# Two attention layers in one kernel: where the projection's results are made and stored, and when the second layer's weights are mixed

## The chip, the cores and the metric

The kernel runs on one core of a Trainium2 chip. The metric is the device time of one execution in microseconds (us). The kernel before the change took 3325.8 us, the median of three runs (3324.72, 3326.9 and 3325.8). The profiled execution spans 3324.6 us. All times below are from that profile, and L12 is line 12 of the kernel's source. The engines are named PE (matrix multiplications; PEld is its loading of weights), DVE (vector engine), ACT (activations), POOL (GpSimd) and SP (which issues all DMAs here).

## What is computed

Two layers of the same form, on x of shape 8 x 512 x 32 x 32 (8 images, 512 channels, 1024 positions), all in float32. For each layer and each image:

```python
xn   = groupnorm(x) * gamma + beta                    # 8 groups in layer 0, 32 in layer 1
q, k, v = split(qkv_w @ xn + qkv_b)                   # 1536 x 512 weights, 8 heads of 64
attn = softmax(q.T @ k / sqrt(64))                    # 1024 x 1024 per head
out  = attn @ v
x    = proj_w @ out + proj_b + x                      # the residual
```

The images are independent of one another, and the second layer reads what the first one wrote.

## The kernel before, in words

A unit is one layer of one image. There are 16: units 0 to 7 are layer 0, units 8 to 15 layer 1. The outer loop (L856) goes over the units and interleaves neighbours: it emits the projections of unit u to q, k and v (`projections`, L451), then the output projection of unit u-1 (`project`, L524), then the attention of unit u (`attention`, L610). The stages of one unit are therefore: q, k, v; the output projection of the unit before it; attention, during which the next unit's group norm is worked out piece by piece.

The order of the instructions on each engine is that in which the code emits them; nothing reorders them afterwards. An engine takes its queue in order and stops at an instruction that waits. Waits come from data dependencies and from tile pools: a pool with n buffers makes the writer of a new tile wait until whoever used that buffer last is done with it.

**The projections.** The multiplications by a weight matrix use Strassen's scheme (Winograd's form) with seven products of half-sized blocks in place of eight; `blocks` (L353) is this for q, k, v and o (the output projection). It needs sums of weight blocks, made once per layer by `mix_weights` (L139, four additions or subtractions for each matrix), and sums of the data, made by `mix_right`. In most units three of the seven products (`INNER`) are themselves done by the scheme, with inner left factors made of the weights by `mix_inner_left` (L216), stored in DRAM and loaded at the end of an attention (`load_inner_left`, L237). Units 0 and 8 multiply the output's matrix without this inner scheme; so do q and k of unit 0, and v in every unit.

In `blocks`, intermediate sums live in three tiles of 128 x 2 x 512: p1 (pool `accpool`, tag "acc"), u2 (pool `trpool`, tag "tr") and u3 (for the output projection: pool `rbpool`, tag "rb"). The callbacks finish the four quarters of the result:

- `c11` (L555) makes the first quarter from PSUM and the residual;
- `others` (L562) adds a sum tile to the PSUM bank for each of the other three quarters (on DVE, L565);
- with the inner scheme, `add_rest` (L408) and `rests` (L571) add what the inner products left over, on POOL (L411, L412, L575), after ACT has copied pieces out of PSUM (L396 to L405);
- `done` (L536) adds bias and residual to u2, u3 and p1 (L532).

The residual w.res is four tiles of 128 x 1024 with tag "p" in `ppool`, which has 4 buffers. The same four buffers hold the exponentials of the attention that follows. Results are stored by `store` (L552) in half rows of 256 KB, eight for each unit, from w.res.

**Attention.** 64 steps in 8 chunks of 8 (`c, t = divmod(s, NT)`, L771). Each step has a pair of score products on PE (L643), one exponential on ACT (L651, into a tile "p"), the product of the previous step's exponential with v (L671), and an addition of the exponential to a running sum on DVE (L688 for the first two of a chunk, L690 for the others). A p tile is free again when PE's product and DVE's addition have read it. At the start of a chunk DVE also evacuates and transposes for the one before (L697, L703), a little later it reduces (L713); in chunks 3, 5 and 7 it works out reciprocals (seven small instructions, L730 to L739, at t = 0) and divides (L753, at t = 6). The running sums take tiles of tag "acc" (2 buffers), the transposes tiles of tag "tr" (2 buffers).

**What is hung into the attention.** `at_step` (L910) is called after each step and emits work for the next unit: mean and variance in chunk 1 (with a power on POOL, L298, at t = 5), seven small scale operations on DVE in chunk 2 at t = 0 (L304 to L316), the normalization on ACT in chunks 2 to 5, and sums for the next unit in chunk 6. In unit 0 all of this comes a chunk later (`late`, L908). It also emits the parts of `mix_inner_left`: one part for each of chunks 3, 4 and 5, at t = 0:

```python
            if t == 0 and 3 <= c < 3 + len(left_parts):
                left_parts[c - 3]()
```

The parts exist in units 0 and 7 (q and k of each layer: 24 POOL operations of 128 x 128 and six stores) and 1 and 9 (the output's matrix: half as many).

**The second layer's weights.** In unit 7 (`u == B - 1`, L883) the kernel loads the three matrices of layer 1 (3 MB) as soon as unit 7's q, k and v no longer need those of layer 0, and emits all twelve mixing operations on POOL at once (L885, L886), ahead of the output projection of unit 6 and of attention 7.

## Time and profile before

| engine | busy us | share of the span | instructions |
|---|---|---|---|
| PE | 3273.6 | 98% | 21776 |
| PEld | 1847.7 | 56% | 21776 |
| DVE | 2446.7 | 74% | 2977 |
| ACT | 1583.0 | 48% | 2065 |
| POOL | 903.5 | 27% | 956 |

| group of instructions | count | mean ns |
|---|---|---|
| L643 PE, scores, 64 x 512 | 7808 | 590 |
| L671 PE, products with v, 64 x 512 | 8192 | 590 |
| L651 ACT, exponential, 128 x 1024 | 976 | 1023 |
| L690 DVE, addition of exponentials, 128 x 1024 | 768 | 1240 |
| L688 DVE, the first addition of a chunk | 128 | 1259 |
| L575 POOL, left-over sums, 128 x 512 | 78 | 1270 (median) |
| L886 POOL, mixing of layer 1's weights, 128 x 512 | 12 | 1257 to 1721 |
| L565 DVE, finishing a quarter of the result, 128 x 512 | 90 | 680 |

DMA is light: a mean of 54 GB/s over the span. A store of a half row takes 2.0 us from issue to landing in the median.

How to read such a profile. The page gives the busy time of each engine, the span in 40 slices (each digit a tenth of the slice; PEclk is the clock that PE was granted), and the chain of work that ended last. A matmul's end is modelled from its start, so PE's busy share is not the share of its peak, and a short wait can be hidden under the end of the matmul before it. The view of waits says which engine waited for which instruction, with the sum, the count and the longest. The timeline lists instructions by time: start, duration, engine, line, what is written and read, and in brackets how long the engine had been idle and what released it.

### The profile page before, as it was taken

Reading aid. Unit: us, or ns where it says so; the run is one execution under the profiler, and the core shown is the slowest. Engines: PE = TensorE matmul, PEld = TensorE weight load, DVE = VectorE, ACT = ScalarE, POOL = GpSimd, SP = SyncE. Lnnn points to the kernel's source line nnn. Section 1 sums busy time; section 2 is a strip of 40 time slices with the busy share of each in tenths; the row PEclk is TensorE's granted clock in tenths of the full one; section 3 lists DMA queues with packets and bytes.
Section 4 is the critical chain, followed back from the end, with each engine's and each line's share of the span. In section 5 each row is a group of like instructions: output and inputs, shape, how many; then the busy total and the mean of one; then the engine's idle time right before and its main releaser. Section 6 shows DMA issues by size and latency. Waiting matters only on the chain.

```text
span 3324.6 us, 54851 instructions
## 1 busy us (share of the span) xinstructions
PE 3273.6 (98%) x21776; PEld 1847.7 (56%) x21776; DVE 2446.7 (74%) x2977; ACT 1583.0 (48%) x2065; POOL 903.5 (27%) x956
## 2 busy tenths in 40 slices
PE   8999999999999999997999999999999999999999
PEld 4445465555646556564465554646556565565643
DVE  4876958769586795965958779586795967859577
ACT  1552726436274462733726436274462734537254
POOL 0231051421504214045251411504214042240510
PEclk9999999999999999998999999999999999999999
DMA  2111110121201212013111111201212012120121
GB/s 78 43 46 70 42 72 28 41 78 36 80 24 35 78 35 90 15 35 115 50 71 42 52 58 43 81 24 35 78 36 90 15 34 84 39 80 15 49 83 47
DMA packets 77525, 178.44 MB, mean 54 GB/s; under 512 B 21968, under 2 KB 26192, under 8 KB 77264
## 3 DMA queue, kind: packets, MB, share of 16 engines
q1 hardware_dynamic: 77264, 174.86, 15.6%
q8 instruction: 177, 2.90, 0.4%
q14 instruction: 84, 0.69, 0.1%
HBM read 135.62 MB, written 37.62 MB: 52 GB/s over the span
## 4 chain that ended last, share of the span: by engine, by line
PE 93%; POOL 3%; DVE 1%; DMA 1%; issue 1%; ACT 1%; SPq 0%; ACTq 0%; POOLq 0%; DVEq 0%
PE a L671 25%; PE s L643 24%; PE a L373 17%; PE s L373 15%; PE a L391 5%; PE s L391 5%; POOL x L575 1%; PE a L643 1%; DMA mid<-x 1%; ACT p L651 0%; DVE acc L690 0%; PE s L591 0%; PE a L591 0%; POOL m_o L411 0%; POOL m_o L412 0%
## 5 line engine op out<-in xcount | busy, mean ns | idle before, releaser
L651 ACT ACTIVATE p<-s 128x1024 f32<-128x1024 f32 x976 | 996.8, 1023 | 561.6 <-PE s L643 502.9
L671 PE MATMUL a<-p,v 64*64 64x512 f32 x8192 | 1120.5, 590 | 9.6 <-ACT p L651 8.5
L643 PE MATMUL s<-q,k 64*64 64x512 f32 x7808 | 1077.3, 590 | 1.4 <-DVE v L517 1.4
L690 DVE TENSOR_TENSOR acc<-acc,p 128x1024 f32<-128x1024 f32 x768 | 952.4, 1240 | 88.6 <-ACT p L651 36.2
L671 PEld LDWEIGHTS a<-p,v 64*64 64x64 f32 x8192 | 403.4, 132 | 492.6 <-ACT p L651 362.4
L643 PEld LDWEIGHTS s<-q,k 64*64 64x64 f32 x7808 | 421.6, 133 | 396.5 <-issue 387.9
L866 POOL TENSOR_TENSOR r<-xn 128x256 f32<-128x256 f32 x60 | 75.0, 1250 | 1154.3 <-DVE acc L690 887.7
L688 DVE TENSOR_TENSOR acc<-p,p 128x1024 f32<-128x1024 f32 x128 | 161.2, 1259 | 29.7 <-ACT p L651 29.7
L298 POOL TENSOR_TENSOR y<-var,half 128x4 f32<-128x4 f32 x16 | 32.2, 2014 | 532.6 <-DVE var L296 532.6
L703 DVE STREAM_TRANSPOSE tr<-acc 128x1024 f32<-128x1024 f32 x128 | 157.9, 1234 | 0.0
L713 DVE TENSOR_REDUCE red<-tr 128x32 f32<-128x1024 f32 x128 | 153.8, 1202 | 0.5
L697 DVE TENSOR_TENSOR ao<-a,tmp 128x512 f32<-128x512 f32 x128 | 87.9, 687 | 63.0 <-ACT tmp L696 62.9
L421 ACT COPY p_o<-a 128x1024 f32<-128x1024 f32 x15 | 15.2, 1012 | 244.2 <-PE a L373 244.2
L373 PE MATMUL a<-xn,w 128*128 128x512 f32 x272 | 125.5, 605 | 4.0 <-DVE xn L326 4.0
L373 PE MATMUL s<-xn,w 128*128 128x512 f32 x256 | 115.4, 594 | 1.7 <-DVE xn L170 1.6
L373 PE MATMUL a<-w,xn 128*128 128x256 f32 x512 | 115.7, 379 | 0.0
L373 PE MATMUL a<-x_t,s1w 128*128 128x512 f32 x256 | 115.1, 592 | 0.0
L373 PE MATMUL s<-x_t,s2w 128*128 128x512 f32 x256 | 115.1, 592 | 0.0
L492 POOL TENSOR_TENSOR k<-k,m_k 128x512 f32<-128x512 f32 x90 | 112.3, 1270 | 0.0
L492 POOL TENSOR_TENSOR q<-q,m_q 128x512 f32<-128x512 f32 x90 | 112.0, 1266 | 0.0
L373 PEld LDWEIGHTS a<-w,xn 128*128 128x128 f32 x512 | 97.4, 190 | 13.5 <-issue 0.5
L320 ACT ACTIVATE xn<-xn,shift,scale 128x512 f32<-128x512 f32 x124 | 99.3, 803 | 6.6 <-DVE shift L316 6.6
(241 smaller groups left out, 4236.0 us busy)
## 6 DMA issues: line engine op xcount, KB each, us to landing
rb<-drec SPq DMA_DIRECT2D x128, 256.0 KB, 3.9
xn<-mid SPq DMA_DIRECT2D x36, 512.0 KB, 7.7
il<-il SPq DMA_DIRECT2D x30, 576.0 KB, 4.4
xn<-x_dram SPq DMA_DIRECT2D x32, 512.0 KB, 7.0
x<-x_dram SPq DMA_DIRECT2D x32, 512.0 KB, 4.8
mid<-x SPq DMA_DIRECT2D x64, 256.0 KB, 2.0
x<-mid SPq DMA_DIRECT2D x28, 512.0 KB, 5.0
out_dram<-x SPq DMA_DIRECT2D x56, 256.0 KB, 2.0
```

Source lines behind the costliest of these rows:

```text
L320: nc.scalar.activation(cols, cols, AF.Identity, bias=st["shift"][:, c : c + 1], scale=st["scale"][:, c : c + 1],)
L373: nc.tensor.matmul(dst, at[:, c, ts(i, P)], moving[:, c, :], start=start and c == 0 and not (tokens and i % 2), stop=stop and c == 1, skip ...
L391: nc.tensor.matmul(dst, left[j], right[j], start=start, stop=stop, skip_group_check=True)
L492: w.last[sel].append(nc.gpsimd.tensor_add(cols, cols, rest[:, i, :]))
L643: nc.tensor.matmul(bank[e * H : (e + 1) * H, j, :], w.k[pr][j * H : (j + 1) * H, t * P + e * H : t * P + (e + 1) * H], w.q[pr][j * H : (j ...
L651: exp = nc.scalar.activation(p, bank, AF.Exp, scale=SCALE)
L671: nc.tensor.matmul(banks[r][j * H : (j + 1) * H, :], w.v[rows, t, lo : lo + D], p[rows, j, :], start=(t == 0), stop=(t == NT - 1),)
L688: nc.vector.tensor_add(acc, state["first"], p)
L690: nc.vector.tensor_add(acc, acc, p)
L697: i1 = nc.vector.tensor_add(w.ao[pr // 2][:, pr % 2, ts(qh, FD)], banks[1], tmp)
L703: nc.vector.transpose(tr, state["acc"].pop(c))
L713: nc.vector.tensor_reduce(red[:, :, qh, :], state["tr"].rearrange("p j (f i) -> p j f i", i=BL), AX.X, ALU.add)
```

## The change

It has three parts.

1. `others` writes the finished quarter into the tile that holds the sum (p1, u2 or u3) instead of the residual tile, `rests` adds to it there, and `store` stores from there. The first quarter stays in the residual tiles. The aim is that the residual tiles, whose buffers the attention's exponentials need, don't have to wait for the stores.
2. The twelve mixing operations of layer 1's weights are not emitted at once in unit 7 but put ahead of the inner left factors' parts, to be emitted one at a time from attention 7's steps. The aim is that they do not stand in front of the output projection's work on POOL.
3. The parts are emitted at every second step (t = 0, 2, 4, 6) from chunk 3 on, and from chunk 4 on in unit 0.

```diff
+        results = {}
+
         def store(o, h):
-            nc.sync.dma_start(dst[o * P : (o + 1) * P, ts(h, FD)], w.res[o][:, ts(h, FD)])
+            nc.sync.dma_start(dst[o * P : (o + 1) * P, ts(h, FD)], results[o, h])
 
         def c11(bank):
             for i in range(2):
-                cols = w.res[i][:, :FD]
+                cols = results[i, 0] = w.res[i][:, :FD]
                 plus(cols, i, bank[:, i, :], cols)
...
         def others(r, h, bank, more):
             for i in range(2):
                 o = 2 * r + i
-                w.evac[h] = nc.vector.tensor_add(
-                    w.res[o][:, ts(h, FD)], bank[:, i, :], more[:, i, :]
-                )
+                results[o, h] = more[:, i, :]
+                w.evac[h] = nc.vector.tensor_add(more[:, i, :], bank[:, i, :], more[:, i, :])
...
         def rests(r, h, rest):
             for i in range(2):
                 o = 2 * r + i
-                cols = w.res[o][:, ts(h, FD)]
+                cols = results[o, h]
                 nc.gpsimd.tensor_add(cols, cols, rest[:, i, :])
                 store(o, h)
...
         if u == B - 1:
             lefts, mixing_w = mix_weights(1, load_weights(1), nc.gpsimd)
-            for part in mixing_w:
-                part()
-        left_parts = ()
+        left_parts = []
         if u in (0, B - 1):
             left_parts = mix_inner_left(units[u + 1][0], lefts[:2], inner_left)
+            if u > 0:
+                left_parts = mixing_w + left_parts
         elif u in (1, B + 1):
...
             c, t = divmod(s, NT)
-            if t == 0 and 3 <= c < 3 + len(left_parts):
-                left_parts[c - 3]()
+
+            if left_parts and t % 2 == 0 and c >= 3 + late:
+                left_parts.pop(0)()
```

## The prediction

> **What bounds the kernel now.** The page first. PE is busy for almost the whole span, and the chain that ended last runs over PE, so a gain can only be PE idle time or throttled clock.

> ```profile
> PE 3273.6 (98%) x21776; PEld 1847.7 (56%) x21776; DVE 2446.7 (74%) x2977; ACT 1583.0 (48%) x2065; POOL 903.5 (27%) x956
> PEclk9999999999999999998999999999999999999999
> PE 93%; POOL 3%; DVE 1%; DMA 1%; issue 1%; ACT 1%; SPq 0%; ACTq 0%; POOLq 0%; DVEq 0%
> ```

> POOL's 3% of the chain is odd, and the clock drops in one slice. The waits of PE, longest first, begin with one of 16.3 us, and a small class of 18 waits for exponentials:

> ```profile
> PE a L391 <- ACT m_o L396: 16.3, 1, 16.3
> PE a L671 <- ACT p L651: 8.5, 18, 2.3
> ```

> The timeline around 1530 us (unit 7, when the projection of unit 6 is due) shows the big one. Columns: start, duration, engine, line, tiles, [idle before <- releaser].

> ```profile
> 1516.98 1.27 POOL L886 TENSOR_TENSOR s1w<-w 128x512 f32<-128x512 f32 x1 [12.92 <-DMA w<-qkv_wT_dram]
> 1518.38 3.44 DVE L532 SCALAR_TENSOR_TENSOR u_o<-x,vec,u_o 128x512 f32<-128x512 f32 x2
> ...
> 1535.16 2.48 POOL L575 TENSOR_TENSOR x<-x,m_o 128x512 f32<-128x512 f32 x2
> 1537.67 0.37 ACT L396 COPY m_o<-a 128x256 f32<-128x256 f32 x1 [23.61 <-POOL x L575]
> 1538.09 1.22 PE L391 MATMUL a<-ro,lo 128*128 128x256 f32 x2 [16.28 <-ACT m_o L396]
> ```

> POOL takes its queue in order: the twelve mixing operations of L886 (waiting for weights until 1516.98, ending at 1533.7) stand ahead of the projection's sums (L411, L412, L575), ACT waits for the tile these free, PE for ACT.

> The 18 small waits lie at the starts of attentions. Unit 6:

> ```profile
> 1322.38 1.95 PE L643 MATMUL s<-q,k 64*64 64x512 f32 x16
> 1324.13 2.17 ACT L651 ACTIVATE p<-s 128x1024 f32<-128x1024 f32 x2 [1.28 <-DMA mid<-x]
> 1324.61 2.51 POOL L575 TENSOR_TENSOR x<-x,m_o 128x512 f32<-128x512 f32 x2
> 1328.08 1.02 ACT L651 ACTIVATE p<-a 128x1024 f32<-128x1024 f32 x1 [1.77 <-DMA mid<-x]
> 1329.25 1.09 PE L671 MATMUL a<-p,v 64*64 64x512 f32 x8 [0.28 <-ACT p L651]
> ```

> The first four p tiles are the residual tiles x; each exponential waits for their stores to land. PE's recorded wait is less than its real loss, as busy time is modelled. I therefore took, from the trace, the time from an attention's first score matmul to its 65th L671 matmul (first product of step 8). Units 0, 1 and 9, whose projection has no POOL part or which have none, take 15.47, 15.50, 15.50 us. Units 2 to 8: 16.33, 16.81, 17.15, 17.03, 16.33, 16.93, 17.08; units 10 to 15: 16.30, 16.35, 16.28, 16.34, 16.29, 16.40. Over 15.50 that is 9.2 + 5.0 = 14.1 us.

> [...] in the DVE and POOL timelines at 222 us:

> ```profile
> 222.19 2.48 POOL L492 TENSOR_TENSOR q<-q,m_q 128x512 f32<-128x512 f32 x2
> 222.33 1.19 DVE L734 TENSOR_TENSOR tot<-one,two 32x64 f32<-32x64 f32 x1
> 223.56 0.23 DVE L735 STREAM_TRANSPOSE rows<-tot 32x64 f32<-32x64 f32 x1
> ```

> L734's median is 0.214 us; beside a 128x512 POOL sum it took 1.19, until that ended; the one-input L735 kept its 0.23. [...] Here the clock was 0.63 in 1520 to 1540 us and 0.95 in the next 20 us, and stayed 1.00 around the 2.3 us wait near 144 us.

> **Part 1, weights mixed during attention 7: the removal.** From the projection's first matmul to the first score, unit 6 takes 1299.48 to 1322.38 = 22.90 us, unit 7 1503.60 to 1544.99 = 41.39. With nothing ahead of its POOL sums unit 7 should match unit 6: -18.5 us, 16.3 of it the wait and 2.2 the slow clock. The weights' DMA stays where it is and still lands near 1517.

> **Part 1, the addition.** Written at every second step from chunk 3 on, the pieces look spread out. But in the changed program's instruction order they follow, on POOL, directly behind the pow of unit 8's norm (L298), and their waits (weights landed, tiles read by PE earlier) are met by then. Nothing holds POOL to the step; before, the pieces written at chunks 3, 4, 5 of unit 7 already ran back to back from the pow's end (1574.17) to 1592.4, in chunk 2. So twelve 128x512 sums, 1.22 us apart (L886, 1531.24 to 1532.46), now run first, then the 24 of 128x128. In the old clock:
> - Sums 1 to 3 go beside L690, L697 and L703 until 1578.6.
> - DVE is then at the seven small scale operations (L304 to L316, two SBUF inputs mostly). Beside 128x128 sums they took 2.45 us (1577.72 to 1580.17), one per POOL operation of 0.41; alone 1.15. Beside 128x512 sums, six waits of 1.22 = 7.2 us, to 1584.95.
> - L688 waits for one sum more, ends near 1587.2 instead of 1581.38, 5.8 late. The exponential of the chunk's fifth step needs the p tile that L688 frees; it was 0.1 late already, and PE had 0.3 us in hand (exponential end to product 0.44 as a rule, 0.15 at least). PE stalls 5.5 us.
> - The last three sums alternate with L690s, each pair some 2.2 us (1.13 of reading and 1.08) against a step of 1.716, and DVE enters chunk 3 about 2.7 us late. There the reciprocals run beside the 128x128 sums: 2.45 us as in unit 0 (137.01 to 139.50) for 1.65 alone. The room is 2.35 + 0.3, so 2.7 + 2.45 - 2.65 = 2.5 us.

> The same rule gives 2.4 for unit 0's chunk 3 (5.1 us from L730 to L688's reading, less 2.65), where PE waited 2.3. With 0.3 for what is left in chunks 5 and 7: +8.3 us. Bounds: 3 if sums and small operations interleave better, 12 with a slow clock after the 5.5 us gap (the 2.2 us of the old stall) and repeats in later chunks. I take 8.3.

> **Part 2, results in the sums' tiles.** The additions are the same in number and size (L565 0.68 us, PSUM and one SBUF input; L575 1.27): 0. The x tiles are now free when DVE has read them (L532, at 1319.1 in unit 6) and the two left halves are stored (POOL done 1313.26, landing some 2.2 later), before the first exponential could start (1322.38 + 1.12 = 1323.5). The wait added: the first sum of probabilities (L688, step 1) takes the tile of p1 and waits for its two stores. Queued behind it on DVE are the L690s; ACT's fifth exponential waits for them. Those stores are what the first two exponentials awaited before: landed by 1325.4, start + 3.0. L688 can't read before start + 4.6 anyway, as L575 holds POOL's read until 1327.02, and may start as late as start + 5.0 without hurting. So it is hidden behind L575. The third tile's stores (u2) have until the second transpose. I take 13.5 of the 14.1 us; bounds 8 (some units keep a wait, moved to DVE) and 14.1.

> **Part 3, left factors later.** On POOL the order is the same in units 0, 1 and 9, so unit 0's wait of 2.3 us stays. Only their DMAs move, to 10 us later, over 40 us ahead of the load that reads them: 0.

> Sum: 3325.8 - 18.5 - 13.5 + 8.3 = 3302.1, taken as 3302.

> **Rivals.** A: [...] POOL is held to the step: 3325.8 - 18.5 - 14.1 = 3293. For it: unit 7 lost nothing in chunk 2 before. Against: those were 0.45 us sums, not 1.26. B: the store wait only changes engine, from ACT to DVE: 3302 + 8 to 13 = 3310 to 3315. For it: DVE is 19.4 us busy of 20 in places. Against: the 2 us above. C: [...] with throttling: 3306 to 3309. D, slower: L688 gets stuck behind late stores in all 14 units. To lose the gain takes 24/14 = 1.7 us each, 2.2 to show as slower: 3333. Stores would need 6 us after their sum where the trace shows 2.2, at worst 3.4.

> **Numbers.** Forecast 0.55, A 0.15, B 0.12, C 0.15, D 0.03. The range 3294 to 3311 leaves out most of A's low end, B's high end and D. The bound of 0.2% is 6.6 us, so all but D and a corner of B are faster: 0.95, 0.03, 0.02.

> **What would show it.** Right: no L391 wait of 16 us and no dip near 1530; 15.5 us to step 8 in units 2 to 15; in unit 7 POOL's twelve sums back to back after L298, small DVE operations of about 1.2 us, and PE waits for p of 5 and 2 us in chunks 2 and 3. Wrong: sums spread over chunks 3 to 5; L688 idle for stores.

## The result and the profile after

The changed kernel takes 3302.75 us (median of four runs, 3301.48 to 3304.32); the kernel before, on the same chip, 3325.28 us. The ratio is 0.9932, with a 95% interval of 0.9914 to 0.9949: 0.7% faster. The prediction was 3302 us with a range of 3294 to 3311. The profiled executions span 3324.6 us before and 3300.8 after, a difference of 23.8 us. So the sum was right. Three of its terms were not, and their errors cancelled.

The page after, in the lines that answer to those that the prediction shows of before (busy times, PE's clock in 40 slices, the chain that ended last):

```profile
PE 3268.8 (99%) x21776; PEld 1767.2 (54%) x21776; DVE 2459.1 (74%) x2977; ACT 1585.3 (48%) x2065; POOL 922.4 (28%) x956
PEclk9999999999999999999999999999999999999999
PE 97%; DVE 2%; issue 0%; ACT 0%; DMA 0%; POOL 0%; SPq 0%; DVEq 0%; ACTq 0%
```

POOL is gone from the chain, and DVE has taken 2% of it in place of 1. The waits of PE after the change:

```profile
PE a L278 <- DVE mv L270: 10.7, 1, 10.7
PE a L672 <- ACT p L652: 7.3, 4, 4.4
PE a L373 <- DVE xn L326: 4.0, 1, 4.0
```

The 16.3 us wait at L391 is gone. The first and third lines belong to the start of the program and were there before (10.9 and 4.0). The waits for an exponential still sum to 7.3 us, against 8.5 before, but there are four in place of eighteen, and the longest is 4.4 us where it was 2.3: the old small ones have gone and a large new one has come. (The additions shift the lines by one: L643 is now L644, L651 is L652, L671 is L672, L688 is L689, L690 is L691, L697 is L698, L703 is L704, L575 is L576.)

To see where the time went, I measured each attention in the matmuls' start times, as in the prediction:

| from the trace, us | before | after | difference |
|---|---|---|---|
| end of attention 6 to first score of attention 7 | 111.42 | 92.98 | -18.4 |
| first score to first product of step 8, units 2 to 8 and 10 to 15, sum over 15.50 | 14.1 | 0.0 | -14.1 |
| attention 7 from step 8 on, over the usual 94.83 | 0.1 | 8.2 | +8.1 |
| attention 0 | 112.88 | 112.90 | 0 |

The three terms sum to -24.4 us. The spans differ by 23.8: attention 0 begins 0.4 us later, and 0.2 us lie in small differences elsewhere.

The timeline at the start of attention 7 shows the first two rows of the table. The columns are those of the prediction's timelines.

```profile
1519.11 2.50 POOL L576 TENSOR_TENSOR p_o<-p_o,m_o 128x512 f32<-128x512 f32 x2
...
1520.82 1.95 PE L644 MATMUL s<-q,k 64*64 64x512 f32 x16
...
1521.98 1.94 ACT L652 ACTIVATE p<-s 128x1024 f32<-128x1024 f32 x2 [0.68 <-PE s L644]
...
1523.80 1.04 ACT L652 ACTIVATE p<-a 128x1024 f32<-128x1024 f32 x1
...
1525.61 1.23 DVE L689 TENSOR_TENSOR acc<-p,p 128x1024 f32<-128x1024 f32 x1 [2.63 <-POOL u_o L576]
```

POOL's sums now run at 1519 instead of 1535, write p_o in place of x, and no exponential waits for a DMA. DVE's first sum of probabilities (L689) waited 2.63 us, behind POOL's L576 on u_o, and PE lost nothing by it.

The new wait lies in chunk 2 of attention 7:

```profile
1548.53 1.98 POOL L918 TENSOR_TENSOR s1w<-w 128x512 f32<-128x512 f32 x1
...
1550.59 1.28 POOL L918 TENSOR_TENSOR s2w<-s1w,w 128x512 f32<-128x512 f32 x1
...
1552.12 1.01 DVE L304 TENSOR_TENSOR y<-y 128x4 f32<-128x4 f32 x1
...
1553.06 1.27 POOL L918 TENSOR_TENSOR s4w<-w,s2w 128x512 f32<-128x512 f32 x1
...
1553.16 1.19 DVE L306 TENSOR_TENSOR w<-y,var 128x4 f32<-128x4 f32 x1
...
1558.20 1.19 DVE L316 TENSOR_TENSOR shift<-vec,ms 128x4 f32<-128x4 f32 x1
...
1559.31 1.21 DVE L689 TENSOR_TENSOR acc<-p,p 128x1024 f32<-128x1024 f32 x1
1559.33 2.32 POOL L918 TENSOR_TENSOR s1w<-w 128x512 f32<-128x512 f32 x1
...
1560.61 1.03 ACT L652 ACTIVATE p<-s 128x1024 f32<-128x1024 f32 x1 [5.62 <-DVE acc L689]
...
1561.78 1.98 PE L672 MATMUL a<-p,v 64*64 64x512 f32 x8 [4.45 <-ACT p L652]
...
1563.51 1.96 PE L644 MATMUL s<-q,k 64*64 64x512 f32 x8
```

The same operations in the kernel before, from the first small one to the sum behind them:

```profile
1577.72 0.33 DVE L304 TENSOR_TENSOR y<-y 128x4 f32<-128x4 f32 x1
...
1580.17 1.21 DVE L688 TENSOR_TENSOR acc<-p,p 128x1024 f32<-128x1024 f32 x1
```

The mixing operations (L918) do run back to back from the end of the pow. Seven DVE operations on 128 x 4 numbers, 0.12 to 0.17 us each in unit 6, take 1552.12 to 1559.31 = 7.2 us: six of them last 1.0 to 1.2 us, and one (L310) kept its 0.16. Before, in the same unit, the seven took 2.45. So L689 begins 4.7 us later than before (7.2 - 2.45), counted from step 8 of its own attention, the exponential that needs its p tile waits for it, and PE stands still. And the two groups of matmuls after the gap start 1.73 us apart instead of 0.86: PE's clock is down. The trace has it at 0.50 from 1560.23 to 1567.06 us.

### The profile page after: what moved, and what is told of

It is laid out like the page before. It is cut to its first block, busy times and chain, and to the rows that moved or that the text cites. A ratio compares the mean times of both kernels' runs of the same rounds, so it can differ in the third digit from the quotient of the medians.

```text
span 3300.8 us, 54815 instructions
## 1 busy us (share of the span) xinstructions
PE 3268.8 (99%) x21776; PEld 1767.2 (54%) x21776; DVE 2459.1 (74%) x2977; ACT 1585.3 (48%) x2065; POOL 922.4 (28%) x956
## 4 chain that ended last, share of the span: by engine, by line
PE 97%; DVE 2%; issue 0%; ACT 0%; DMA 0%; POOL 0%; SPq 0%; DVEq 0%; ACTq 0%
PE a L672 26%; PE s L644 25%; PE a L373 17%; PE s L373 15%; PE a L391 6%; PE s L391 6%; PE a L644 1%; PE s L592 0%; PE a L592 0%; DVE acc L691 0%; ACT p L652 0%; DMA xn<-x_dram 0%; DVE tr L704 0%; DVE acc L689 0%; PE a L278 0%
## 5 line engine op out<-in xcount | busy, mean ns | idle before, releaser
L652 ACT ACTIVATE p<-s 128x1024 f32<-128x1024 f32 x976 | 999.1, 1025 | 567.5 <-PE s L644 528.4
L672 PE MATMUL a<-p,v 64*64 64x512 f32 x8192 | 1095.9, 590 | 7.3 <-ACT p L652 7.3
L644 PE MATMUL s<-q,k 64*64 64x512 f32 x7808 | 1053.3, 591 | 1.4 <-DVE v L517 1.4
L691 DVE TENSOR_TENSOR acc<-acc,p 128x1024 f32<-128x1024 f32 x768 | 965.9, 1258 | 74.0 <-ACT p L652 20.6
L672 PEld LDWEIGHTS a<-p,v 64*64 64x64 f32 x8192 | 376.4, 131 | 511.8 <-ACT p L652 360.2
L644 PEld LDWEIGHTS s<-q,k 64*64 64x64 f32 x7808 | 372.3, 133 | 446.6 <-issue 438.0
L298 POOL TENSOR_TENSOR y<-var,half 128x4 f32<-128x4 f32 x16 | 32.2, 2014 | 508.4 <-DVE var L296 508.4
L689 DVE TENSOR_TENSOR acc<-p,p 128x1024 f32<-128x1024 f32 x128 | 156.0, 1219 | 21.0 <-ACT p L652 14.6
L704 DVE STREAM_TRANSPOSE tr<-acc 128x1024 f32<-128x1024 f32 x128 | 158.0, 1234 | 0.0
L698 DVE TENSOR_TENSOR ao<-a,tmp 128x512 f32<-128x512 f32 x128 | 88.0, 687 | 64.2 <-ACT tmp L697 64.0
L492 POOL TENSOR_TENSOR k<-k,m_k 128x512 f32<-128x512 f32 x90 | 112.3, 1268 | 0.0
L492 POOL TENSOR_TENSOR q<-q,m_q 128x512 f32<-128x512 f32 x90 | 112.1, 1267 | 0.0
```

Of the source, the lines that this page charges most:

```text
L492: w.last[sel].append(nc.gpsimd.tensor_add(cols, cols, rest[:, i, :]))
L644: nc.tensor.matmul(bank[e * H : (e + 1) * H, j, :], w.k[pr][j * H : (j + 1) * H, t * P + e * H : t * P + (e + 1) * H], w.q[pr][j * H : (j ...
L652: exp = nc.scalar.activation(p, bank, AF.Exp, scale=SCALE)
L672: nc.tensor.matmul(banks[r][j * H : (j + 1) * H, :], w.v[rows, t, lo : lo + D], p[rows, j, :], start=(t == 0), stop=(t == NT - 1),)
L689: nc.vector.tensor_add(acc, state["first"], p)
L691: nc.vector.tensor_add(acc, acc, p)
```

## The experiments

The times are medians, except that of the fills, which is one run. "Attention 7" is the time from its first score to its last product; 110.33 us is what nearly every attention takes in the changed kernel. Each experiment ran on one chip with the kernel before, which took 3326.72 us beside the two halves, the fills and the held parts; 3327.28 beside the left factors alone, the halved operations and the windows; and 3326.05 beside the last two. The changed kernel ran beside none of them, so a difference of a few us between versions is read from the traces, and the times only have to agree with it.

### The two halves of the change, each alone

Here "results" is the edit of `store`, `c11`, `others` and `rests` alone, made on the kernel before:

```diff
-                w.evac[h] = nc.vector.tensor_add(
-                    w.res[o][:, ts(h, FD)], bank[:, i, :], more[:, i, :]
-                )
+                results[o, h] = more[:, i, :]
+                w.evac[h] = nc.vector.tensor_add(more[:, i, :], bank[:, i, :], more[:, i, :])
```

> Results in the sums' tiles alone; mixing and left factors as before. My account (waits at the starts of 14 attentions, 14.1 us in all, go; the projection of unit 6 still stalls 18.4): 3325.3 - 14.1 = 3311 us, first score to first product of step 8 at 15.5 us in every unit. Rival (the two parts overlap, the store wait also played a role in the big stall): more than 16 us faster, or, if the wait only moved to DVE, less than 8.

"Mixing" is the rest of the diff (with the later place of the left factors), also on the kernel before:

```diff
-            for part in mixing_w:
-                part()
...
+            if u > 0:
+                left_parts = mixing_w + left_parts
...
+            if left_parts and t % 2 == 0 and c >= 3 + late:
+                left_parts.pop(0)()
```

> Mixing during attention 7 and the later left factors, results stored from the residual tiles as before. My account: -18.4 for the projection, +8.2 inside attention 7: 3315 us, attention starts at 16.3 to 17.1 us as before. Rival (the loss of 8.2 in attention 7 comes from the results' new tiles or their stores): attention 7 loses nothing and the time is near 3307.

Measured: results alone 3312.79 us, 13.9 less than before (ratio 0.9959, 0.9945 to 0.9974); mixing alone 3317.3 us, 9.4 less (0.9971, 0.996 to 0.9982). Together 23.3, and the whole change gave 22.5: within the intervals, some 4 to 6 us to each side, the halves add up. The traces say it more sharply. With results alone, PE's waits were these:

```profile
PE a L391 <- ACT m_o L396: 15.8, 1, 15.8
PE a L278 <- DVE mv L270: 11.1, 1, 11.1
PE a L373 <- DVE xn L326: 4.0, 1, 4.0
PE a L672 <- ACT p L652: 2.3, 1, 2.3
```

Seventeen of the eighteen waits for an exponential have gone, and that left is unit 0's; every unit has 15.47 or 15.50 us to step 8. The large wait at L391 stays. With mixing alone the large wait is gone, attention 7 is 8.3 us too long beyond its late start, and the small waits stay. Neither rival holds in the traces: the removal of the store wait is worth its full 14 us and doesn't turn into another wait, and the move of the mixing gains 18 and gives 8 back.

### The left factors' place alone

```diff
-            if t == 0 and 3 <= c < 3 + len(left_parts):
-                left_parts[c - 3]()
+            if left_parts and t % 2 == 0 and c >= 3 + late:
+                left_parts.pop(0)()
```

> Edit of the kernel before: part 3 alone (the inner left factors' parts written at every second step from chunk 3 on, in unit 0 from chunk 4 on). My theory, that POOL is not held to the step and its order stays: unit 0's wait of 2.3 us in chunk 3 stays, attention 0 stays at 112.9 us, the time is that of the kernel before, 3325 to 3327. Rival, that the later place frees chunk 3: attention 0 becomes 110.4 to 111.5, the time 3323.5 to 3325.

Measured: 3326.53 us, ratio 1.0 (0.9991 to 1.0008); attention 0 took 112.88 us, as before. Writing the parts at a later step moves nothing on POOL: its operations in unit 0 start at the same distance from the first score, within 0.02 us.

### Is it the reading of SBUF that costs 8 us?

In the changed kernel, the twelve mixing operations become fills of the same tiles by the same engine, in the same places of its queue (the second layer's mixed weights are then left out):

```diff
-                left_parts = mixing_w + left_parts
+                left_parts = [
+                    partial(nc.gpsimd.memset, part.args[0], 0.01) for part in mixing_w
+                ] + left_parts
```

> The changed kernel with each of the twelve mixing operations replaced by a fill of the same output tile with a constant, so POOL writes as much at the same place but reads nothing; the second layer's weights are wrong, the q, k and v of layer 1 with them. If the loss of 8.2 us in attention 7 comes from POOL and DVE excluding each other at reading SBUF: attention 7 falls from 118.6 to 110.5 to 111.5 us and the time to 3295. If it comes from POOL's work as such, from its writes or from where it stands in the queue: 118 us and 3302.

Measured: 3294.86 us (a single run), 7.9 below the changed kernel's 3302.75, and attention 7 exactly 110.33. In its timeline the fills stand beside the same small operations:

```profile
1552.81 0.52 POOL L920 MEMSET s1w<- 128x512 f32 x1
...
1552.85 0.16 DVE L306 TENSOR_TENSOR w<-y,var 128x4 f32<-128x4 f32 x1
...
1553.05 0.31 DVE L308 TENSOR_SCALAR h<-w 128x4 f32<-128x4 f32 x1
```

A fill reads nothing, and L306 is back at 0.16 us: it began and ended while a fill was running. The fills are also shorter (0.52 us), but they stood beside all seven, and of these only L308 took more than its usual time, by 0.14 us. What a sum does and a fill doesn't is to read: beside a sum L306 took 1.19 us, beside a fill of the same size 0.16. POOL waits in its turn: its ninth sum, which began with L689 in the changed kernel, took 2.32 us in place of 1.27 and ended 1.13 us after L689 did.

### Per instruction or per byte?

```diff
+    def halves(part):
+        for i in range(2):
+            part.func(*(t[:, i] for t in part.args))
...
-                left_parts = mixing_w + left_parts
+                left_parts = [
+                    partial(halves, part) for part in mixing_w
+                ] + left_parts
```

> Edit of the changed kernel: each of the twelve mixing operations of 128x512 is done as two of 128x256, so that the same bytes are read in 24 instructions. My theory, that a small DVE operation waits for whatever single POOL instruction is reading, and so pays per instruction: the seven scale operations of chunk 2 cost some 0.7 us each instead of 1.2, the gap of PE in chunk 2 falls from 4.7 to about 2.3 us, too short for the slow clock of 2.6 us, and the reciprocals in chunk 3, now beside the last halves, cost some 3.4 us. Unit 7's attention is 5 to 6.5 us over 110.33 instead of 8.2, the time 3299.5 to 3301. Rival, that it is the sum of reading time that counts: the same sum is read, attention 7 stays 8 us over, the time stays at 3303.

Measured: 3301.32 us, ratio 0.9922 to before (0.9907 to 0.9938). That is 1.4 us under the changed kernel, too little to tell by the time. In the trace attention 7 is 6.6 us too long instead of 8.2, just above what I had expected (5 to 6.5) and not the rival's 8. The timeline (the additions shift these lines by four more):

```profile
1553.01 0.65 DVE L310 TENSOR_TENSOR w<-y,var 128x4 f32<-128x4 f32 x1
...
1553.70 0.67 DVE L312 TENSOR_SCALAR h<-w 128x4 f32<-128x4 f32 x1
...
1560.10 1.99 PE L676 MATMUL a<-p,v 64*64 64x512 f32 x8 [2.53 <-ACT p L656]
...
1561.83 1.88 PE L648 MATMUL s<-q,k 64*64 64x512 f32 x8
...
1563.53 1.04 PE L676 MATMUL a<-p,v 64*64 64x512 f32 x8
```

The small operations do pay one POOL instruction each: 0.65 us where it was 1.19. PE's wait falls to 2.53 us. But I had expected the clock to stay up after so short a wait, and it didn't: two groups ran at 1.73 and 1.70 us, a loss of 1.7. In chunk 3 the reciprocals took 3.0 us (expected 3.4), and PE lost 1.2.

### Held to the step

In rival A of the prediction, POOL was to be held to the step at which a part is written. Here it is, by a dependency of each part's first operation on that step's exponential:

```diff
...
-                left_parts.pop(0)()
+                held = left_parts.pop(0)()
+                tc.add_manual_dep(
+                    getattr(held, "ins", held), name_of(state["exp"][-1]), DEP, reason="held to its step"
+                )
```

> The changed kernel with each part held to its step: the first operation of a part also waits for the exponential of the step that emits it. If the loss comes from the sums standing beside the seven scale operations at once, and spreading them as the code reads is the cure: attention 7 at 110.5 to 111.5, 3295 us or, with unit 0's wait of 2.3 gone too, 3293. If every 1.1 us of a sum's reading is taken from DVE, which has little to spare in chunks 3, 5 and 7: the loss comes back in smaller pieces there, some 4 to 6 us in attention 7, no slow clock, and 2 saved in unit 0: 3298.

Measured: 3304.79 us, ratio 0.9933 to before (0.9916 to 0.9949): no gain over the changed kernel, and neither of my two expectations. Unit 0's wait nearly went (attention 0: 111.44), but attention 7 takes 121.91 us, 11.6 too long where the changed kernel has 8.2. Its loss is spread: 1.9 us in chunk 4, 2.5 in chunk 5, 1.8 in chunk 6 and 5.3 in chunk 7, where PE's longest wait of 3.0 us brings the slow clock too. DVE and POOL at the turn from chunk 4 to 5 (lines shifted by two):

```profile
1585.40 10.61 DVE L693 TENSOR_TENSOR acc<-acc,p 128x1024 f32<-128x1024 f32 x6
...
1595.93 0.68 DVE L700 TENSOR_TENSOR ao<-a,tmp 128x512 f32<-128x512 f32 x1
1595.95 1.28 POOL L920 TENSOR_TENSOR s2w<-s1w,w 128x512 f32<-128x512 f32 x1 [2.34 <-ACT p L654]
```

Six sums of probabilities take 10.6 us, 1.77 each, where PE's step is 1.716; normally it is 1.30 (four in 5.19 us in unit 6). DVE enters chunk 5 3.2 us behind ACT's copy of the PSUM (which ended at 1592.73). By the windows view of the changed kernel, DVE is busy 12.1 to 13.4 of 13.73 us in the chunks 2 to 7 of unit 6, so a chunk has at most 0.3 to 1.6 us to spare. Spreading POOL's sums didn't help here, as they were spread over DVE's two-input sums; in the changed kernel only the first and the last four of the twelve meet them (POOL took 1.98 us for that first one and 2.19 to 2.32 for the last four, 1.26 to 1.28 for the others).

### In the windows of one-input work

DVE has two operations with one SBUF input at the start of each chunk, 1.2 us each: the transposition (now L706) and the reduction (L716). In the changed kernel, where one of each ran beside POOL's sums in chunk 2, no transposition took more than 1.24 us and no reduction more than 1.22. Here each of the eight mixing operations of q and k is held behind the DVE operation just ahead of one of these, in chunks 1 to 4; v's four go to unit 8's projections; the left factors' parts are held behind the first sum of chunks 4, 5 and 6:

```diff
...
-            if left_parts and t % 2 == 0 and c >= 3 + late:
-                left_parts.pop(0)()
+            for part in held_parts.get((c, t), ()):
+                held = part()
+                on = state["free"][(c + 1) % 2][1] if t == 0 else state["summed"]
+                tc.add_manual_dep(getattr(held, "ins", held), name_of(on), DEP, reason="held")
...
+        if u == B - 1:
+            rest.setdefault(9, []).extend(mixing_w[8:])
```

> Edit of the changed kernel: of the twelve mixing operations the eight of q and k are each held, by a dependency, behind a DVE operation of attention 7 after which DVE has one-input work (the transposition at t = 0 or the reduction at t = 1) in chunks 1 to 4; the four of v are moved into unit 8's projections; the parts of the inner left factors are held in the same way to t = 1 of chunks 4, 5 and 6. My theory, [...]: attention 7 is 110.4 to 111.5 us, unit 0's wait is 0 to 0.7 instead of 2.3, the time 3292 to 3295. Rival, that the kernel has no room for POOL's reading anywhere in an attention (holding the same operations to their steps gave 3304.8, with attention 7 at 121.9): attention 7 stays 5 us or more over 110.33, the time at 3299 or above.

Measured: 3298.43 us, ratio 0.9913 (0.99 to 0.9927): between the two expectations. (Unit 0's wait in chunk 3 is gone but for 0.4 us, and attention 0 takes 111.80 us, since it now loses 1.0 in chunk 7.) In its timeline (lines shifted by two), a window:

```profile
1550.47 1.23 DVE L706 STREAM_TRANSPOSE tr<-acc 128x1024 f32<-128x1024 f32 x1
...
1550.63 1.28 POOL L923 TENSOR_TENSOR w<-w 128x512 f32<-128x512 f32 x1 [2.45 <-DVE ao L700]
...
1551.63 0.30 DVE L306 TENSOR_TENSOR y<-y 128x4 f32<-128x4 f32 x1
...
1551.96 0.16 DVE L308 TENSOR_TENSOR w<-y,var 128x4 f32<-128x4 f32 x1
```

The eight mixing operations now cost next to nothing: up to step 40 (the start of chunk 5) attention 7 stands at 70.66 us, and undisturbed units at 70.61. But it ends 4.5 us too long: PE's product is 1.9 us late in chunk 5 and 2.4 in chunk 7. For chunk 5 the timeline of the DMA queue and of DVE has the cause (lt holds the partial sums of softmax, il the stored left factors):

```profile
1588.60 3.95 SPq L234 DMA_DIRECT2D il<-l  x2
...
1592.64 1.81 SPq L722 DMA_DIRECT2D lt<-red  x3
...
1594.39 0.21 DVE L733 TENSOR_TENSOR one<-red,lt 32x64 f32<-32x64 f32 x1 [1.49 <-DMA lt<-red]
```

### The order on SP

The small transfers of lt leave only after the stores of the left factors, which wait for POOL. What they carry was ready at 1582.69, when the reduction (L716) ended; the two stores went out at 1588.60 and 1592.22, each 0.03 us after the POOL operation that it stores (L233) had ended, and lt at 1592.64. That SP stood at the second store with lt behind it was my reading of these times, an estimate. To try that, the parts are written two steps later, with the same dependency, so that POOL's order stays and lt comes ahead of the stores on SP:

```diff
-        held_parts = {(4 + i, 1): [part] for i, part in enumerate(left_parts)}
+        held_parts = {(4 + i, 3): [part] for i, part in enumerate(left_parts)}
```

> Edit of e7_windows: the parts of the inner left factors are written two steps later (t = 3 instead of t = 1 of chunks 4, 5 and 6), with the same dependency, so that POOL's order is unchanged and only SP's order changes: the stores of a part come behind the three small transfers of softmax sums (lt) instead of ahead of them. My theory of the 1.9 us that e7_windows lost at the start of chunk 5 of attention 7 is that SP stood at the part's stores, which wait for POOL until 1592, with the transfer of the sums behind them, for which DVE then waited (1.49 and 1.08 us): that stall falls to 0.5 or less, and attention 7 from 114.8 to 112.5 to 113.5 us; time 3296 to 3297. Rival, that the 1.9 us are DVE's lost time beside POOL's small operations: the stall in chunk 5 stays at 1.5 to 2, time 3298 to 3299.

The same timeline after that:

```profile
1581.67 1.81 SPq L722 DMA_DIRECT2D lt<-red  x3
...
1587.56 3.95 SPq L234 DMA_DIRECT2D il<-l  x2
...
1590.65 1.24 DVE L706 STREAM_TRANSPOSE tr<-acc 128x1024 f32<-128x1024 f32 x1
...
1591.80 0.17 DVE L733 TENSOR_TENSOR one<-red,lt 32x64 f32<-32x64 f32 x1
```

Measured: 3295.05 us, ratio 0.9908 (0.9892 to 0.9925). The intervals of the two versions overlap; the traces, with POOL's operations at the same places of attention 7 up to chunk 5, decide. lt now leaves at 1581.67, L733 waits for nothing, and chunk 5 costs nothing (13.74 us). SP's order was the cause: lt left 0.02 us after its reduction had ended (1581.65), where it had left 9.95 us after. Chunk 7 gained too, which I hadn't expected: its late product fell from 2.4 to 1.7 us, and in unit 0 from 0.8 to none. Attention 7 is 112.08, attention 0 110.70. A wait of 1.7 us in chunk 7 of attention 7 is left, in which DVE comes late out of chunk 6, where it has two sums for the next unit besides.

Last, the same with everything earlier (two mixing operations in chunk 0, six in the windows of chunks 1 to 3, the left factors of unit 0 in chunks 1, 2 and 4, those of units 1 and 9 not held):

```diff
...
+            places = ((1, 0), (2, 3), (4, 3)) if u == 0 else ((4, 3), (5, 1), (6, 3))
+        else:
+            places = ((3, 0), (4, 0), (5, 0))
...
+            for at, part in zip(((0, 4), (0, 6), (1, 0), (1, 1), (2, 0), (2, 1), (3, 0), (3, 1)), mixing_w):
```

> Edit of e9_after_sums: everything earlier, so that less falls in chunks 6 and 7, in which DVE has least to spare. Two of the eight mixing operations go to the fifth and seventh step of chunk 0, the other six to the one-input windows of chunks 1 to 3; in unit 7 the parts of the left factors go behind the evacuation in chunks 4 and 6 and the first sum in chunk 5; in unit 0 to chunks 1, 2 and 4; in units 1 and 9 they are not held. My theory, that POOL's reading costs the end only what DVE can't spare in that chunk: attention 7 is 110.4 to 112.0 us, attention 0 110.3 to 110.8, time 3292.5 to 3295. Rival, that a part of eight small operations costs its 2 us wherever it stands: attention 7 stays at 112.5 to 114, attention 0 at 111.5, time 3296 to 3297.5.

Measured: 3294.36 us, ratio 0.9905 (0.9888 to 0.9921). Attention 7 is 112.12, as with the version before it, and attention 0 111.18, which is 0.5 longer than there: earlier places alone brought nothing in these two, against my expectation. One part still stands in chunk 6 of attention 7 (1.4 us late in chunk 7), and 0.4 us were lost in its chunk 1; attention 0 lost 0.5 in chunk 2. Units 1 and 9 gained back the 0.4 us each that holding their parts had cost. This is the fastest version, some 8 us under the changed kernel; that it beats the one before it isn't shown, as their runs overlap.

## Why the prediction was right

The parts are numbered as in the prediction.

**Part 1, the removal: right.** Predicted -18.5 us with unit 7 matching unit 6; measured -18.4 (92.98 us from attention to attention, where other units have 92.95).

**Part 2: the sum right, 0.6 us low; what hides the new wait was wrong.** Predicted -13.5 of 14.1; measured all 14.1, in 13 attentions (not 14, as rival D and the first expectation count). The prediction put the wait for p1's stores behind L575 (now L576), which was to hold L688 (now L689) to 4.6 us after the first score. Only unit 7 went that way (4.8 us). In the other twelve L689 came ahead of L576 on u_o, 3.2 to 3.5 us after the first score. In ten of them the exponential was the last thing that it waited for, so the stores had landed by then. In two (12 and 15) it was the DMA, after 1.26 and 2.48 us of idling, and L689 began 3.5 us after the first score at the latest (unit 15: 3160.16 - 3156.71), well inside the 5.0 us that the prediction allowed. PE lost nothing. Rivals B and D fall by this and by the run of results alone.

**Part 3: right.** 0, and unit 0's wait stayed at 2.3 us.

**Part 1, the addition: the sum right (8.3; measured 8.2), three terms wrong.** That small DVE operations wait for POOL's reading, one instruction at a time, is shown by the fills and the halves (L306 took 1.19 us beside a sum, 0.16 beside a fill and 0.65 beside half a sum). The terms:

- Chunk 2: predicted a stall of 5.5 us. That the small operations would take 7.2 us came out (though its six waits of 1.22 sum to 7.3). The step that failed is "L688 waits for one sum more": it came first at 1559.31 and POOL waited for it (2.32 us instead of 1.27). Measured 4.7 us in place of 5.5.
- The slow clock, which the prediction had only in its bounds: measured 2.6 us, three groups of matmuls 1.71 to 1.73 us apart. This belonged in the sum: in the trace of before the clock had stayed at 1.00 around a wait of 2.3 us and dropped with one of 16.3, so nothing there spoke for full clock after the prediction's own stall of 5.5.
- Chunk 3: predicted 2.5 us, from a DVE 2.7 late. While PE was slow DVE caught up: it began L698 0.7 us later against the product of step 24 than in unit 6 (1572.13 against 1571.29; 1360.78 against 1360.65), the reciprocals took 2.28 us (2.45 predicted), and PE lost 0.5. With 0.7 in place of 2.7, the prediction's own formula gives 0.5 (0.3 with the measured 2.28 as well).

The remaining 0.3 was 0.4, in chunk 7. So the errors are -0.8, +2.6, -2.0 and +0.1 us, and that they cancel was luck: the prediction left the slow clock out of the sum, and its absence made chunk 3 too dear by about as much. The two may go together, as time that PE loses is time in which DVE catches up. The run of mixing alone agrees: after a product as late as here (4.68 us) the slow clock cost it 2.3 instead of 2.6, and chunk 3 1.2 instead of 0.5. But no run has the same stall at full clock, so this is argued and not shown.

Rival C had the throttling right and the total too high (3306 to 3309). Rival A's 3293 us allowed nothing for the work added to attention 7. As it stands in the changed kernel it cost about 8 us (the fills in its place took 7.9 us less), and with POOL held to the step the time was 3304.79 us.

## What to carry to other kernels

Ask of every operation that is moved to "free" time of POOL what DVE does beside it: a chain of tiny DVE operations paid nearly a whole POOL instruction each here (1.19 us in place of 0.16), while a transposition beside one kept its 1.23 us and a reduction its 1.21. An order in the source doesn't hold an engine to a time: look for the instruction ahead of it in its own queue, and, where work is held back by a dependency, at what stands behind its DMAs on the issuing queue (lt left 9.95 us late behind such stores, and DVE waited 1.49 us for it). When a stall is long enough for the clock to drop, put the drop into the sum (2.6 us after the stall of 4.68 here), and allow for the engines behind it catching up meanwhile.

## What was not expected of the hardware

The clock drops after a shorter gap than I had thought. Late products in attentions, measured from when they were due (the start of the score group before plus 0.86 us), with what the groups after them lost:

| kernel, chunk | product late, us | groups at some 1.7 us | lost to the clock, us |
|---|---|---|---|
| windows, 7 | 2.40 | none | 0 |
| held, 5 | 2.40 | none | 0 |
| before, unit 0, 3 | 2.58 | none | 0 |
| halves, 2 | 2.76 | two | 1.7 |
| held, 7 | 3.18 | two | 1.7 |
| mixing alone, 2 | 4.68 | two, and one of 1.40 | 2.3 |
| after, 2 | 4.68 | three | 2.6 |

Counted within the step just before each drop, PE was idle for 2.4 to 3.1 of the 3.41 us (an estimate from the traces, with PE idle from when the product was due until it came); the gaps above without a drop, all split between two steps, had at most 2.0 us in one. So a limit on the idle time within a step fits these gaps as well as a limit on lateness, and no run here tells the two apart. If it holds, the same gap brings a drop or not by where it falls.

Also, the one-input L308 (TENSOR_SCALAR, 128 x 4) waited like its neighbours with two inputs: 1.20 us in the changed kernel and 0.67 with halves, against 0.17 alone. The transpositions and reductions have one input too and kept their times beside the same sums (at most 1.24 and 1.22 us). What sets L308 apart from them no run here shows.
